# Graph attention on one core: more buffers for the terms of q, loads and one-hots moved, and last units begun in idle buffers

## The chip, the core and the metric

The kernel runs on one NeuronCore of a Trainium2 chip. The core has five engines, each with its own instruction stream: TensorE (PE, matrix products), VectorE (DVE, elementwise work and reductions), ScalarE (ACT, elementwise work), GpSimd (POOL) and SyncE (SP, which here only issues transfers). Work on different engines meets through semaphores; each stream is worked off in order. Times are microseconds (us) on the device. A time given for a kernel is the median of several runs; the profile is one further execution.

## The reference, cut to what matters

There are N = 12,500 nodes with 128 features and E = 212,500 edges, sorted by destination. Eight heads have 16 features each.

```
h   = relu(layernorm(x))
q,v = h Wq' + bq,  h Wv' + bv          per node
k   = edge_attr Wk' + bk               per edge
three logits per edge and head:  q[src].k,  q[dst].k,  q[src].q[dst]   (each times 1/4)
score = sum of their three softmaxes over the edges of a destination, times edge_weight**lam
out = x + leaky_relu( (sum over a node's edges of score * v[dst]) Wo' + bo, 0.1 )
```

Since v is taken at the destination, it is constant within a node's sum: a node needs only the sums of weighted and of plain exponentials for its 24 logits (three kinds of eight heads), and its own v.

## The kernel before

Edges are cut into 416 blocks of 512. The blocks form five streams (S = 5) of neighbouring edges; a step t takes one block of each stream, so there are T = 84 steps and 420 block slots, numbered g = 5 t + s. On each engine the order of work is the order in which the program writes it: `pin` ties each instruction to the one before it on its engine.

**First stage (from the start to about 88 us).** The nodes' rows are loaded, normalized, turned and multiplied by Wq (`statistics`, `scale`, `rectify`, `turn_h`, `nodes_q`), and q is stored to `q_table` in DRAM. Between these groups of four node tiles stand pieces of edge work (`edges_1` to `edges_4`): source indices are turned, and the destination's place within a block (`rel_d`) and flags and weights (`fa_d`) are stored to DRAM. Afterwards the program starts the gathers of the first nine blocks (`gather`, line 625: four indirect transfers of 128 rows of q a block, issued by POOL) and the loads of edge features of the first six blocks (`fetch_edges`).

**Terms of q (about 85 to 155).** `terms_q` writes each value of q as a sum of three bf16 terms: ACT casts (line 845), DVE subtracts (846), ACT casts the rest (851), DVE subtracts (852), and SP stores the group's 384 KB to `q3_table` (854). This is done for 25 groups of four tiles in tiles `q3` with three buffers. In the middle (g = 12) `edges_5` stands in one piece: a reduction (756), a product (758) and four turns of 104 columns into `ends`.

**Main loop.** For a block, PE turns the edge features (`turn`, 1068) and multiplies them by Wk (`project`, 1076 and 1078). The destination's q needs no gather: destinations are sorted, so a window of 42 nodes from `q3_table` (`win`) is spread over the block's edges by a product with one-hots (`spread_q`, 1087), which ACT makes from `relb` (`one_hots`, 1062 and 1063). ACT copies the spread rows to the gathered tile `qq` (1089). DVE forms the three products and their sums over 16 features (`logits`, 1097, 1098, 1100). Once per step, for all five blocks together: the logits are turned (`turn_logits`), a running maximum is taken (`scan_max`: 1130, 1133), ACT takes exponentials (`powers`, 1141 to 1146; PE spreads the weights, `att_ps`, 1148), DVE runs two sums (`scan_sums`: 1154, 1158), marks the last edge of each node (`select`, 1167), and PE and ACT turn the sums back (`turn_sums`) and pick the nodes' rows (`to_rows`, 1191 and 1196), which SP stores to `sums` in DRAM (`put_rows`).

POOL's gathers run LOOK = 9 blocks ahead, in QQ = 11 buffers of `qq`. Gather g waits for products of block g - 9, which keeps it close behind them:

```
if (g - LOOK, j) in behind:
    tc.add_manual_dep(rows.ins, behind[g - LOOK, j], ...)
```

SP's queue holds, in the program's order, the edge loads six blocks ahead, the loads of a step two steps ahead (`fetch`: relb, five fa, register loads, five win), the row stores and the nodes' loads and stores. PSUM tiles of the small parts share three buffers (`small`).

**Nodes.** A unit is 256 nodes; an object `Nodes` holds two. Twenty pairs are finished inside the loop, from step 18 on (`nodes_between`): load sums and x, normalize (970), scores (976 to 981), turn (985, 987), product with Wv, weigh (997), turn, product with Wo, then slope and addition: ACT copies (1007), DVE takes max(0.1 o, o) (1008) and adds x (1009). The nine units left (18, 9, 10, 19, 28, 29, 38, 39, 48; five `Nodes`) are done after the loop, in PSUM tiles of their own (h_ps, v_ps, u_ps, o_ps); six of these nine have sums from two streams, the second loaded into `more` and added (963). Their x is loaded during the last five block slots of the loop.

Of the kernel before, what the change touches and what calls it, by code (L numbers as in the profile page):

```python
# [20 lines left out]
SLOPE = 0.1  # L21
# [451 lines left out]
def ordered_path(ctx: ExitStack, tc: tile.TileContext, flag, x, src, dst, edge_attr, edge_weight,  # L473
# [134 lines left out]
    qqs, st, eas, behind = {}, {}, {}, {}  # L608
# [40 lines left out]
    with tc.tile_pool(name="prep", bufs=1) as prep, \  # L649
# [52 lines left out]
        def turn_edges(of, to):  # L702
            cols = of.rearrange("r (a p j) -> r a j p", a=RB, j=JN)
            for a in range(RB):
                t_ps = prep_ps.tile([P, JN, RW], F32, name="t_ps")
                for j in range(JN):
                    pin(nc.tensor.transpose(t_ps[:, j, :], cols[:, a, j, :], ident[:RW, :RW]))
                pin(nc.vector.tensor_copy(to[:, a:NB:RB, :], t_ps.rearrange("p j r -> p r j")))
# [10 lines left out]
        def of_tile():  # L719
            return prep.tile([RW, RC], BF, name="of", bufs=2)  # L720
# [13 lines left out]
        def edges_3():  # L734
# [6 lines left out]
            rel_b = prep.tile([RW, RB, BE], BF, name="rel_b")  # L741
# [11 lines left out]
        def edges_5():  # L753
            bad = got["bad"] = prep.tile([RW, 1], F32, name="bad")
            step = got["step"]
            pin(nc.vector.tensor_reduce(bad, step[:, :RC], AX.X, ALU.min))
            last = step[:, 1:]
            pin(nc.vector.scalar_tensor_tensor(last, last, 0.0, rel, op0=ALU.is_gt, op1=ALU.mult))
            turn_edges(last, ends)
# [79 lines left out]
        def terms_q(g):  # L839

            if g < GN:
                n = len(tiles_of(g))
                q = xq[:, g * JN:g * JN + n, :]
                q3 = q3s[g] = node.tile([P, JN, 3, F], BF, name="q3", bufs=3)[:, :n]
# [45 lines left out]
        for g in range(AHEAD):  # L890
            fetch_edges(g)
        for g in range(GN + 1):
            terms_q(g)
            if g == GN // 2:
                edges_5()
# [30 lines left out]

    fin = ctx.enter_context(tc.tile_pool(name="fin", bufs=2))
# [11 lines left out]
    class Nodes:  # L939
# [3 lines left out]
        def __init__(self, of):  # L943
            self.of = of
            self.n = 2 * len(of)

        def load_x(self):
            self.x = fin.tile([P, JN, F], F32, name="x_in", bufs=5)
# [3 lines left out]
        def load_sums(self):  # L952
            self.ab = fin.tile([P, JN, 2 * H3], F32, name="ab", bufs=3)
            for i, u in enumerate(self.of):
                for j, t in enumerate(parts_of(u)):
                    to = self.ab
                    if j > 0:
                        to = self.more = fin.tile([P, JN, 2 * H3], F32, name="more", bufs=3)
                    pin(nc.sync.dma_start(to[:, 2 * i:2 * i + 2, :].rearrange("p k c -> p (k c)"),
                                          units(sums[t], u, 1, 2 * H3)[:, 0, :]))  # L960
                    if j > 0:
                        both = self.ab[:, 2 * i:2 * i + 2, :]
                        pin(nc.vector.tensor_add(both, both, to[:, 2 * i:2 * i + 2, :]))

        def normalize(self, lo, hi):
            if lo == 0:
# [6 lines left out]
        def scores(self):  # L973
            n = self.n
            den, num = self.ab[:, :n, 0:H3], self.ab[:, :n, H3:]
# [7 lines left out]
        def turn(self, to):  # L983
            for b in range(self.n):
                pin(nc.tensor.transpose(to[:, b, :], self.h[:, b, :], ident))  # L985
            self.hT = fin.tile([P, JN, P], F32, name="hT")
# [8 lines left out]
        def project_v(self, to):  # L995
            self.product(to, bv3, wv)
            pin(nc.vector.tensor_mul(  # L997
# [5 lines left out]
        def project_o(self, to):  # L1003
# [3 lines left out]
            pin(nc.scalar.copy(o, to[:, :n]))  # L1007
            pin(nc.vector.scalar_tensor_tensor(o, o, SLOPE, o, op0=ALU.mult, op1=ALU.max))  # L1008
# [19 lines left out]
    with tc.tile_pool(name="work", bufs=2) as work, \  # L1028
            tc.tile_pool(name="scan", bufs=2) as scan, \
            tc.tile_pool(name="ps", bufs=1, space=PSUM) as ps:  # L1030
        ks, eTs, qds, lTs, base_v = {}, {}, {}, {}, {}
        end = S * T

        def block_rows(t):
            lo = t if t < G else t - 1
            return lo, slice(0, S * G) if t < G else slice(1, S * G + 1)

        def fetch(t):

            if t >= T:  # L1040
                return
            at, part = block_rows(t)
            relb = load.tile([K3, S, BE], BF, name="relb")
            pin(nc.sync.dma_start(relb, rel_d[part].rearrange("(s b) e -> s b e", b=G)
                                  [None, :, at, :].to_broadcast([K3, S, BE])))
            fa = load.tile([4 * S, BE], BF, name="fa", bufs=4)
            for s in range(S):
                pin(nc.sync.dma_start(fa[4 * s:4 * s + 4], fa_d[s * G + t]))
            _, base_v[t] = nc.values_load_multi_w_load_instructions(
                bases[0:1, t, 0:S], engines=[mybir.EngineType.SP], min_val=0, max_val=N - 1,  # L1050
                skip_runtime_bounds_check_because="the indices of nodes are below N")
            win = load.tile([K3, S, F], BF, name="win")
            for s in range(S):
                pin(nc.sync.dma_start(win[:, s, :], q3_table[bass.ds(base_v[t][s] * 3, K3), :]))
            st[t] = dict(relb=relb, fa=fa, win=win)

        def one_hots(t, s):

            if s == 0:
                st[t]["oh"] = work.tile([K3, S, BE], BF, name="oh")  # L1060
            d = st[t]["relb"][:, s, :]
            pin(nc.scalar.activation(d, d, AF.Abs, bias=before[:K3]))  # L1062
            pin(nc.scalar.activation(st[t]["oh"][:, s, :], d, AF.Relu, bias=1.0, scale=-1.0))  # L1063
# [19 lines left out]
        def spread_q(g):  # L1083
            s, d = g % S, st[g // S]
            qd_ps = ps.tile([P, JN, F], F32, name="qd_ps")
# [264 lines left out]
```

## Time and profile before

| | us |
|---|---|
| median of 3 runs | 2341.86 (2341.75 to 2342.19) |
| the profiled execution's own time | 2333.37 |
| its span, first to last instruction | 2331.5 |

| engine | busy us | share of the span |
|---|---|---|
| DVE | 2150.8 | 92% |
| PE | 1812.6 | 78% |
| POOL | 1658.1 | 71% |
| ACT | 1522.1 | 65% |

A busy share is a mean over stages. In the listings in order of time a line has the start, the duration, the engine, the program's line, the operation, what is written and read, and in brackets how long the engine sat idle before it and what released it. A stretch lists, after its length, the busy time of PE, of weight loads, DVE, ACT and POOL with counts, then PE's granted clock as a share of full, the mean share of the DMA engines, and GB/s. A wait is put down to the releaser that came last; of two merged in one row it may name the wrong one. The issue of a transfer is not counted as busy on SP, but a gather's preparation is on POOL.

### The profile page before, as it was taken

The page shows a single profiled execution, that of the slowest core. Times are in us where ns is not written, and L with a number is a line of the kernel's source. Part 1 is how long each engine was busy: PE and PEld are TensorE (multiplying, and loading weights), DVE is VectorE, ACT ScalarE, POOL GpSimd, SP SyncE. Part 2 cuts the span into 40 slices and gives each one's busy share as a digit, 9 for nine tenths or more (in the row PEclk, how much of TensorE's full clock was granted, in tenths as well). Part 3 has the DMA queues.
Part 4 walks back from the last instruction along what each step waited for, and adds up shares of the span by engine and source line. Part 5 has one row for each costly group of instructions (what it writes and reads, how often), then busy time and mean ns, then how long its engine had stood idle before and what let it go on. Part 6 is the DMA issues. An engine that isn't in the chain of part 4 may idle for free. (4 is left out here: it accounts for less than half of the span.)

```text
span 2331.5 us, 35994 instructions
## 1 busy us (share of the span) xinstructions
PE 1812.6 (78%) x10629; PEld 1415.8 (61%) x10629; DVE 2150.8 (92%) x2263; ACT 1522.1 (65%) x2797; POOL 1658.1 (71%) x1715
## 2 busy tenths in 40 slices
PE   5327888888788888878878778888887777888775
PEld 4315666666666666666666566666666666666654
DVE  7659999999999999999999999999999999999983
ACT  5547676666766676666676676667666667667653
POOL 3547777777777777777777777777777777777740
PEclk9757777777778787787777787778687888688777
DMA  7657545555555555555555655554555554554522
GB/s 201 215 172 197 148 135 148 143 144 149 141 136 159 138 141 163 139 139 154 146 138 139 164 138 140 156 144 137 158 142 140 153 154 135 153 154 134 149 54 60
DMA packets 306681, 341.04 MB, mean 146 GB/s; under 512 B 137667, under 2 KB 225496, under 8 KB 306165
## 3 DMA queue, kind: packets, MB, share of 16 engines
q1 hardware_dynamic: 244906, 222.99, 32.5%
q0 software_dynamic: 54448, 112.96, 19.9%
q10 hardware_dynamic: 7120, 2.70, 0.4%
q8 instruction: 85, 1.39, 0.2%
q14 instruction: 122, 1.00, 0.1%
HBM read 307.79 MB, written 30.64 MB: 145 GB/s over the span
## 5 line engine op out<-in xcount | busy, mean ns | idle before, releaser
L625 POOL DMA_INDIRECT qq<-q_table,src_i x1680 | 1623.4, 966 | 548.6 <-issue 341.4
L1100 DVE TENSOR_REDUCE lT<-prod 128x96 f32<-128x1536 f32 x420 | 736.2, 1753 | 14.4
L1078 PE MATMUL k_ps<-wk,eT 128*128 128x128 f32 x3360 | 613.3, 338 | 103.6 <-ACT eT L1070 95.4
L1078 PEld LDWEIGHTS k_ps<-wk,eT 128*128 128x128 f32 x3360 | 518.9, 236 | 263.7 <-ACT eT L1070 180.9
L1089 ACT COPY qq<-qd_ps 128x512 f32<-128x512 f32 x420 | 245.4, 584 | 548.9 <-PE qd_ps L1087 432.2
L1098 DVE TENSOR_TENSOR prod<-qq,k_ps 128x1024 f32<-128x1024 f32 x420 | 509.8, 1214 | 0.5 <-PE k_ps L1078 0.5
L1087 PE MATMUL qd_ps<-win,oh 126*128 126x128 bf16 x1680 | 203.4, 257 | 213.4 <-DVE prod L1097 173.1
L1068 PE MATMUL eT_ps<-ident,ea 128*128 128x128 f32 x1680 | 342.0, 341 | 2.9 <-DVE found L901 2.9
L1097 DVE TENSOR_TENSOR prod<-qq,qd_ps 128x512 f32<-128x512 f32 x420 | 284.3, 677 | 47.4 <-ACT qq L1089 34.6
L1087 PEld LDWEIGHTS <-oh 126*128 126x128 bf16 x1680 | 159.5, 116 | 257.5 <-issue 208.4
L1062 ACT ACTIVATE relb<-relb,before 126x512 bf16<-126x512 bf16 x420 | 306.3, 729 | 7.4 <-DMA relb<-rel_d 7.4
L1070 ACT COPY eT<-eT_ps 128x512 f32<-128x512 f32 x420 | 246.9, 588 | 50.3 <-PE eT_ps L1068 48.7
L1063 ACT ACTIVATE oh<-relb 126x512 bf16<-126x512 bf16 x420 | 264.6, 630 | 13.4
L1068 PEld LDWEIGHTS eT_ps<-ident,ea 128*128 128x128 f32 x1680 | 243.0, 181 | 3.2 <-DVE found L901 3.2
L1178 PE MATMUL b_ps<-ident,sum 120*128 120x120 f32 x672 | 141.1, 342 | 94.8 <-ACT l L1120 92.3
L1076 PE MATMUL k_ps<-b,ones 3*128 3x512 bf16 x420 | 190.8, 454 | 5.0 <-DVE prod L1098 4.8
L1191 PE MATMUL w_ps<-back,sel 128*126 128x144 f32 x1344 | 186.9, 295 | 0.6 <-ACT back L1179 0.6
L1178 PEld LDWEIGHTS b_ps<-ident,sum 120*128 120x128 f32 x672 | 101.3, 215 | 138.6 <-ACT l L1120 111.4
L1191 PEld LDWEIGHTS w_ps<-back,sel 128*126 128x126 f32 x1344 | 178.4, 197 | 0.8 <-ACT back L1179 0.8
L1179 ACT COPY back<-b_ps 128x480 f32<-128x480 f32 x168 | 97.6, 581 | 47.0 <-PE b_ps L1178 47.0
L1130 DVE TENSOR_TENSOR_SCAN u<-l,u,far_ps 120x512 f32<-120x512 f32 x83 | 105.5, 1271 | 0.8 <-ACT l L1120 0.8
L1158 DVE TENSOR_TENSOR_SCAN sum<-keep,sum,up 120x512 f32<-120x512 f32 x83 | 105.9, 1276 | 0.0
(170 smaller groups left out, 1735.4 us busy)
## 6 DMA issues: line engine op xcount, KB each, us to landing
ea<-in_edge_attr_dram SPq DMA_DIRECT2D x419, 256.0 KB
relb<-rel_d SPq DMA_DIRECT2D x84, 630.0 KB
qq<-q_table,src_i POOLq DMA_INDIRECT x1680
win<-q_table SPq DMA_DIRECT2D x420, 31.5 KB
q_table<-q SPq DMA_DIRECT2D x24, 384.0 KB
fa<-fa_d SPq DMA_DIRECT2D x420, 4.0 KB
sums<-rows SPq DMA_DIRECT2D x416, 7.9 KB
q_table<-xq SPq DMA_DIRECT2D x24, 256.0 KB
```

Source lines behind the costliest of these rows:

```text
L625: rows = pin(nc.gpsimd.indirect_dma_start(out=qq[:, j, 0, :], out_offset=None, in_=q_table, in_offset=bass.IndirectOffsetOnAxis(ap=src_i[: ...
L1062: pin(nc.scalar.activation(d, d, AF.Abs, bias=before[:K3]))
L1063: pin(nc.scalar.activation(st[t]["oh"][:, s, :], d, AF.Relu, bias=1.0, scale=-1.0))
L1068: pin(nc.tensor.transpose(eT_ps[:, j, :], eas[g][:, j * F:(j + 1) * F], ident))
L1070: pin(nc.scalar.copy(eT, eT_ps))
L1078: pin(nc.tensor.matmul(k_ps[:, j, :], eTs[g][:, j, :], wk, start=False, stop=(j == JN - 1)))
L1087: pin(nc.tensor.matmul(qd_ps[:, j, :], d["oh"][:, s, j * P:(j + 1) * P], d["win"][:, s, :], start=(j == 0), stop=(j == JN - 1)))
L1089: pin(nc.scalar.copy(qqs[g][:, :, 1, :], qd_ps))
L1097: pin(nc.vector.tensor_mul(prod[:, :, 2, :], qqs[g][:, :, 0, :], qds[g]))
L1098: pin(nc.vector.tensor_mul(prod[:, :, 0:2, :], qqs[g], ks[g][:, :, None, :].to_broadcast([P, JN, 2, F])))
L1100: pin(nc.vector.tensor_reduce(lTs[t][:, :, s, :], prod.rearrange("p j i (h d) -> p j (i h) d", d=DIM), AX.X, ALU.add))
L1191: pin(nc.tensor.matmul(w_ps[:, i].rearrange("p s c -> p (s c)"), d["sel"][:, j, lo:lo + 3, :].rearrange("p s w -> p (s w)"), d["back"][:, ...
```

## The change

The parts, in order of the program:

- `q3` has four buffers of its own and takes every third group in one of the two buffers of `of` (made 128 partitions tall); `rel_b` uses `of` too, in place of a tile of its own.
- `edges_5` is cut into six pieces, one after every third group of `terms_q`.
- `fetch` is split: relb, fa and the register loads in `fetch`, the win loads in `fetch_rows`. `fetch(0)` stands ahead of `terms_q`.
- At the start of the loop one block's one-hots are made ahead of the first spread, in place of five; `project(0)` and `spread_q(0)` stand ahead of `turn(1)`. In the loop one-hots are made three blocks ahead, in place of five, in five tiles of one block in place of two of five.
- `att_ps` stands first in `powers`, and `powers` ahead of `to_rows`.
- In `project_o` ACT multiplies by the slope while it copies, and DVE takes the maximum against PSUM.
- The nine last units are begun from nine slots before the loop's end (`begin_rest`): their x, h, hT and later their sums lie in buffers of `qq` that no gather uses any more; their products with Wv are kept in PSUM tiles of the loop (`held`), one per slot from the first slot after the last block. After the loop only sums, scores, weighing, the turn, the product with Wo and the store are left; the second sums are loaded on ACT's queue.

```diff
+    def fetch(t):
+        if t >= T:
+            return
+        at, part = block_rows(t)
+        relb = load.tile([K3, S, BE], BF, name="relb")
+        pin(nc.sync.dma_start(relb, ...))
+        fa = load.tile([4 * S, BE], BF, name="fa", bufs=4)
+        for s in range(S):
+            pin(nc.sync.dma_start(fa[4 * s:4 * s + 4], fa_d[s * G + t]))
+        _, base_v[t] = nc.values_load_multi_w_load_instructions(
...
+        st[t] = dict(relb=relb, fa=fa)
+
+    def fetch_rows(t):
+        if t >= T:
+            return
+        win = st[t]["win"] = load.tile([K3, S, F], BF, name="win")
+        for s in range(S):
+            pin(nc.sync.dma_start(win[:, s, :], q3_table[bass.ds(base_v[t][s] * 3, K3), :]))
...
-            rel_b = prep.tile([RW, RB, BE], BF, name="rel_b")
+            rel_b = of_tile().rearrange("r (a e) -> r a e", a=RB)
...
+        def edges_5(i):
             step = got["step"]
             last = step[:, 1:]
+            if i == 0:
+                bad = got["bad"] = prep.tile([RW, 1], F32, name="bad")
+                pin(nc.vector.tensor_reduce(bad, step[:, :RC], AX.X, ALU.min))
+            elif i == 1:
+                pin(nc.vector.scalar_tensor_tensor(last, last, 0.0, rel, op0=ALU.is_gt,
+                                                   op1=ALU.mult))
+            elif i < 2 + RB:
+                turn_edges(last, ends, [i - 2])
...
-                q3 = q3s[g] = node.tile([P, JN, 3, F], BF, name="q3", bufs=3)[:, :n]
+                if g % 3 == 2:
+                    q3 = prep.tile([P, JN, 3, F], BF, name="q3", tag="of", bufs=2)
+                else:
+                    q3 = node.tile([P, JN, 3, F], BF, name="q3", bufs=4)
+                q3 = q3s[g] = q3[:, :n]
...
+        fetch(0)
         for g in range(GN + 1):
             terms_q(g)
-            if g == GN // 2:
-                edges_5()
+            if g % 3 == 2:
+                edges_5(g // 3)
...
-            pin(nc.scalar.copy(o, to[:, :n]))
-            pin(nc.vector.scalar_tensor_tensor(o, o, SLOPE, o, op0=ALU.mult, op1=ALU.max))
+            pin(nc.scalar.activation(o, to[:, :n], AF.Copy, scale=SLOPE))
+            pin(nc.vector.tensor_max(o, o, to[:, :n]))
             pin(nc.vector.tensor_add(y, o, y))
...
+        def one_hots(g):
+            if g < end:
+                oh = ohs[g] = work.tile([K3, BE], BF, name="oh", bufs=5)
+                d = st[g // S]["relb"][:, g % S, :]
+                pin(nc.scalar.activation(d, d, AF.Abs, bias=before[:K3]))
+                pin(nc.scalar.activation(oh, d, AF.Relu, bias=1.0, scale=-1.0))
...
+        starts, holds = (0, 1, 3, 4, 6), ("eT_ps", "eT_ps", "k_ps", "k_ps", "qd_ps")
+        late, turned = {}, {2: (0, 1), 5: (2, 3), 7: (4,)}
+        def spare():
+            return gath.tile([P, JN, 2, F], F32, name="qq").rearrange("p j i f -> p (j i f)")
+        def halves():
+            return spare().rearrange("p (i j f) -> i p j f", i=2, j=JN)
+        def begin_rest(at):
+            if at in turned:
+                late.update(zip(turned[at], halves()))
+            if at in (LOOK - 1, LOOK):
+                late[at - LOOK] = spare()
+            for r, (of, begin) in enumerate(zip(rest, starts)):
+                if at == begin:
+                    to, of.h = halves()
+                    of.load_x(to)
+                if at == begin + 2:
+                    of.normalize(0, 4)
+                if at == begin + 3:
+                    of.hT = late[r]
+                    of.turn(small([P, JN, P], "node_ps"))
+                if at == LOOK + r:
+                    of.held = ps.tile([P, JN, F], F32, name=holds[r], bufs=2 if r < 4 else 1)
+                    of.product(of.held, bv3, wv)
...
-        fetch(0)
+        fetch_rows(0)
         fetch(1)
-        for s in range(S):
-            one_hots(0, s)
+        fetch_rows(1)
+        one_hots(0)
         turn(0)
+        project(0)
+        spread_q(0)
         turn(1)
-        spread_q(0)
-        project(0)
+        one_hots(1)
+        one_hots(2)
         for g in range(end + 2 * S):
...
-            if t + 1 < T:
-                one_hots(t + 1, s)
+            one_hots(g + 3)
...
             elif s == 2:
+                later(powers, t - 1)
                 later(to_rows, t - 2)
-                later(powers, t - 1)
             elif s == 3:
                 later(scan_sums, t - 1)
-                if t + 2 < T:
-                    fetch(t + 2)
+                fetch(t + 2)
+                fetch_rows(t + 2)
...
             nodes_between(t, s)
+            begin_rest(g - (end - LOOK))
...
+        for r, of in enumerate(rest):
+            of.load_sums(*[late[k][:, r * JN * 2 * H3:(r + 1) * JN * 2 * H3].rearrange(
+                "p (j c) -> p j c", j=JN) for k in (-1, 0)])
+        for r in range(len(rest) + 2):
+            if r < len(rest):
+                rest[r].scores()
+                rest[r].weigh(rest[r].held)
+            if 0 <= r - 1 < len(rest):
+                rest[r - 1].turn(small([P, JN, P], "node_ps"))
+            if 0 <= r - 2:
+                rest[r - 2].project_o(small([P, JN, F], "node_ps"))
+                rest[r - 2].store()
```

## The prediction, made before the changed kernel ran

> **What bounds it.** I read the busy shares by stage first: VectorE (DVE) is busy 96 to 98% in the long middle and 40 to 70% at both ends.
>
> ```profile
> 100.00:120.00 20.00, 0.00 (x0) 0.00 (x0) 11.19 (x19) 9.12 (x17) 15.43 (x16) 0.50 0.68 220
> 140.00:160.00 20.00, 0.00 (x0) 0.00 (x0) 12.53 (x33) 7.06 (x14) 6.01 (x6) 0.50 0.66 210
> 300.00:400.00 100.00, 82.88 (x486) 64.24 (x486) 97.97 (x90) 69.47 (x124) 75.91 (x80) 0.78 0.51 141
> 2280.00:2300.00 20.00, 11.21 (x48) 8.05 (x47) 6.99 (x23) 8.04 (x20) 0.31 (x1) 0.67 0.40 109
> ```
>
> (Columns: stretch, length, busy us of PE, weight loads, DVE, ACT, POOL; clock, DMA share, GB/s.) DVE's 97.97 suggests DVE. POOL's 75.91 misleads: 80 gathers per 100 us are all that fit. In order of time POOL reads:
>
> ```profile
> 91.66 1.08 POOL L625 DMA_INDIRECT qq<-q_table,src_i  x1 [10.94 <-DMA ea<-in_edge_attr_dram]
> 146.59 0.94 POOL L625 DMA_INDIRECT qq<-q_table,src_i  x1 [0.30 <-issue]
> 173.73 0.94 POOL L625 DMA_INDIRECT qq<-q_table,src_i  x1 [26.20 <-PE k_ps L1078]
> 174.98 0.95 POOL L625 DMA_INDIRECT qq<-q_table,src_i  x1 [0.30 <-PE eT_ps L1068]
> 2251.76 0.94 POOL L625 DMA_INDIRECT qq<-q_table,src_i  x1 [0.30 <-issue]
> ```
>
> A gather takes 0.94 and 0.30 follows: 1.25, four to a block, 5.0. From 173.73 to 2252.70 POOL never waits beyond this 0.30: 1640 gathers in 2078.97, 1.268 each. So **gather issue is the bound of the loop**; DVE needs less: by the pitches of its rows 3.5 a block plus 5.8 per five blocks (scans 1.9 and 3.0, sel 0.9), so 4.7, and 5.05 where Nodes add 1.85 per five; it trails the gathers. The only hole is 147.53 to 173.73: gather 41, the first of block 10, waits for the products of block 1 (look-ahead of 9).
>
> Next the waits of the stage ahead: 33.8 us of ACT's waits there are for q3_table stores, three q3 buffers.
>
> ```profile
> ACT q L845 <- DMA q_table<-q: 33.8, 21, 8.4
> ```
>
> Then the end, on DVE:
>
> ```profile
> 2262.06 1.75 DVE L1100 TENSOR_REDUCE lT<-prod 128x96 f32<-128x1536 f32 x1
> 2274.03 0.69 DVE L1154 TENSOR_TENSOR ew<-up,att_ps 120x512 f32<-120x512 f32 x1 [5.89 <-ACT up L1145]
> 2292.50 0.26 DVE L963 TENSOR_TENSOR ab<-ab,more 128x96 f32<-128x96 f32 x1 [13.15 <-DMA more<-sums]
> 2323.92 0.42 DVE L1009 TENSOR_TENSOR x_in<-h,x_in 128x256 f32<-128x256 f32 x1 [0.46 <-DVE h L1008]
> ```
>
> The last block's reduce ends near R = 2263.7; the tail from R to 2331.5 is 67.8.
>
> **Start, part by part.** Six q3 buffers for three. Stores now pace 2.28 each (two per 4.56, the casts at 102.06 and 106.90 among others), with or without gathers beside them, so latency sets it. Doubled, latency allows 1.14; DVE needs 1.20 (two subtractions at 0.60 pitch); DMA: stores took 167 GB/s at about 0.48 share (0.68 less 0.20, the gathers' queue's 19.9% in the queue table), so 0.8 share gives 280 GB/s, 1.40 for 384 KB. I take 1.5, DMA-bound; ends 1.4 and 2.28. Splitting the step on ends removes its cluster (119.97 to 128.50, a gap in the stores); its 7 us of DVE fit in the slack, 24.5 x 1.2 + 7 = 36.5 against 24.5 x 1.5 = 36.8.
>
> The first loads (relb, five fa, register loads) go ahead of the stores on SP: 0.54 + 1.93 + 1.3 = 3.8 of issue, 630 KB of transfer, so the first store leaves at 95.5 for 91.5. Last store issued 95.5 + 36.8 = 132.3, landed 135 (2.8 each now). Then only five win loads precede: landing 3.8 after issue at most (159.46 to 163.22), 139. In place of 7.4 of waiting for relb and ten one-hot instructions (161.8 to 168.2), PE does one spread (0.6), a turn (1.06), copies and project(1) (2.7): products of block 1 at **144** for 173.4; DVE starts at 140 for 169.8.
>
> POOL is then not ready: 40 gathers take until 147.5. Here a rule speaks against the change: the Trainium skill, GPSIMD Engine Reference, Specifications, says that POOL shares its SBUF interfaces with DVE and contends with DVE instructions that have two SBUF inputs. The trace agrees, instruction by instruction:
>
> ```profile
> 122.42 2.98 POOL L625 DMA_INDIRECT qq<-q_table,src_i  x1 [0.30 <-issue]
> 122.28 2.29 DVE L758 SCALAR_TENSOR_TENSOR step<-step,dst_r 104x2048 f32<-104x2048 f32 x1
> ```
>
> Over all 1680 gathers, those that begin inside such an instruction are longer than 0.94 by 40 us together (sel 20.9, gap 7.5, terms' subtractions 4.1, L1008 2.3, L758 2.0); those inside one with a PSUM input by nothing. Packed subtractions: 49 x 0.6 / 1.25 = 24 gathers hit, at 0.24 (17 hit now cost 4.1), 5.8 for 4.1: gather 41 at **149**. By the row alone (contention as now) 147.5; I take 149. The start gives POOL 173.7 - 149 = **24.7**. Five us of cover remain; the stall returns once stores exceed 1.7.
>
> **Loop.** The new slope step: ACT scales in its copy (0.58 as before), DVE takes the maximum against PSUM (0.68, as L1097, for 0.68). Its only worth is the 2.3 of gather time that L1008 cost. The rest costs nothing while gathers bound:
> One-hots, same two instructions (1.36), three blocks ahead for five: ACT is 69% busy; without that cover, 1.36 a block. Relb's buffer is now released at a block's second step, just before SP asks for it; SP then sits 9.3 per five blocks (728.3 over 78 waits) at win anyway. Powers (2.1 of ACT) ahead of rows: rows are late by 2.1, the rows' stores on SP come two blocks later; behind them wait edge loads six blocks ahead. In early staging rel_b shares the `of` buffers; POOL's casts may slip 2, ahead of a 10.94 wait.
>
> In the last nine blocks SP waits for an idle qq buffer before loading x (edge loads behind it have four blocks' room); the memset of unit 48 stands behind the last gather on POOL, and its x load, with row stores nobody awaits behind it, lands about 3 later, ahead of its normalization. Five x 0.4 x 4 of ACT and 18 transposes (some 4.5 of PE) enter nine blocks of 5: I charge 1. Loop end: 24.7 + 2.3 - 1 = **26** earlier.
>
> **Tail.** Powers ahead of rows would let ew start at about R + 7 for R + 10.3. But PE is given five products before that chain's end, two ahead of att_ps. From the trace:
>
> ```profile
> 2263.87 1.11 PE L1113 MATMUL l_ps<-ident,lT 128*120 128x128 f32 x4 [6.82 <-DVE lT L1100]
> 2268.38 3.62 PE L1191 MATMUL w_ps<-back,sel 128*126 128x144 f32 x16
> 2272.79 1.16 PE L992 MATMUL node_ps<-wo,hT 128*128 128x128 f32 x8
> 2278.60 3.71 PE L1191 MATMUL w_ps<-back,sel 128*126 128x144 f32 x16 [0.65 <-ACT back L1179]
> ```
>
> A product costs 1.5 at full clock (with its bias), 2.6 at half. The Trainium skill, TensorE: Matmul & The Clock Gate, Part 1, says some 3.4 us of sustained work restore full clock; here PE restarts at 2263.87 and the granted clock stays 0.50 to 2270, 0.64 over 2270:2272, so 7.4. By the page the first product is warm and everything after 3.5 earlier; I take the row: cold to R + 7.5. PE then: l, far, b to R + 3.7; last unit's turn 4.2; product 6.8; turn 7.8; product 9.4; att 9.8 (ew at R + 10.2, gain nothing); w_ps 2.1 warm, 11.9; three products (1.5, 1.5, 0.9) and the old pair's (1.5), 17.3; b_ps 18.8; copy 19.4; w_ps 21.5; rows R + 22 for R + 20.7.
>
> From rows to the first score it is 8.1 now (2284.44 to 2292.50: SP's issue of five row stores, one x load, two ab and one more, then 3.6 to land). The x load (0.25) goes, and the second sums (0.42) to ACT's queue: 7.4, R + 29.4 for 28.8. Then DVE alone: per Nodes scores 2.0 (2292.50 to 2294.5), weigh 0.6, max and add 1.3, 18 for four and a half; the v products and turns that it waited among are gone. I add 1.8 where the first output product (turn 1.06, copy 0.58, cold 2.7, ACT 0.58) is late, and 2.5 of drain at the end: R + 51.7 for R + 60.6; the 7.2 from there to the span's end stay. Tail **8.9** shorter, between 0 (PE cold throughout: 9 more) and 13.
>
> **Sum:** 26 + 8.9 = 34.9 of the profiled 2333.37 (span 2331.5): 2298.5. The runs' median is 8.5 above that execution, so I subtract from the median: 2341.86 - 34.9 = **2307**.
>
> **Rivals.**
> (1) The buffers don't help: stores keep 2.28 (the DMA queues, not latency). Last store 95.5 + 55.9 = 151.4, products of block 1 at 163, the start gives 10.7 for 24.7: 2321. For: 384 KB are large; against: share 0.68, and 306 GB/s at 90:95.
> (2) The early products only move: PE stays cold through the tail, rows at R + 31, the tail gives nothing: 2316. For: the clock was 0.5 to 0.77 in most of 2262:2300; against: PE would have no gap.
> (3) Slower: PE becomes the loop's bound. It is busy 82.9 of 100 at clock 0.78; after the reordering a lower clock would have it pass the gathers' 5.07 a block: it takes the 34.9 back (1.7% of the loop's 2075) where the mean clock falls to 0.636 (0.78 x 0.829 / 1.017), and at 0.63 (2.6%, 55 us) it ends at 2362. Against: PE's order changes little, and fuller PE ran warmer.
>
> **Chances.** Likeliest case 0.63, 2307 (its own 2299 to 2313); (1) 0.13; (2) 0.17; (3) 0.04; 0.03 for still faster (2294). To hold 0.8 the range needs the first, most of (2), some of (1): 2297 to 2320. A measurement tells about 0.2%, 4.7 us: faster 0.94, same 0.02, slower 0.04.
>
> **What would show it.** Gather 41 near 149 with no wait above 0.3 (right) or a wait for k_ps (stores too slow); stores about 1.5 apart; first L1097 near 140; last gather near 2226; no gather longer than 0.94 inside the maximum; ew still some 10 after the last reduce, and w_ps near 2.1; last add about 52 after it. The prediction is wrong if gathers wait in mid-loop, or if DVE's lag behind the last gather (11 to R) grows.

## The result and the profile after

The changed kernel takes **2306.3 us** (median; 2304.05 to 2308.75) where the kernel before, measured beside it, takes 2342.03: a ratio of 0.9844, 95% interval 0.983 to 0.9859, 35.7 us. The forecast was 2307.0. The profiled execution of the changed kernel took 2308.75 (span 2307.0), 2.4 above its median, while that of before lay 8.7 below its own (2342.03); so the two traces show only 24.6 of the 35.7, and a total is compared below by medians, a stage by traces. In the runs e1 to e8 below each engine paused for some 1 to 5 us about every 12 us of the loop, for every kernel (before: 2915 to 2933), so that of them only the stages outside the loop and ratios on the same chip are read.

Three of the stretches shown for before, with the same columns (stretch, length, busy us of PE, weight loads, DVE, ACT, POOL; granted clock, DMA share, GB/s):

```profile
100.00:120.00 20.00, 3.93 (x17) 2.72 (x17) 16.52 (x29) 14.71 (x27) 15.73 (x15) 0.50 0.96 337
300.00:400.00 100.00, 83.57 (x481) 64.13 (x481) 97.76 (x89) 67.51 (x121) 76.29 (x78) 0.77 0.51 148
2280.00:2300.00 20.00, 14.01 (x55) 10.08 (x55) 14.26 (x36) 5.49 (x10) 0.00 (x0) 0.59 0.14 46
```

While the terms of q are stored, all transfers together now move 337 GB/s at a share of 0.96 where they moved 220 at 0.68, and DVE is busy 16.52 of 20 us where it was 11.19. The middle is as it was; the gain lies at the two ends. ACT's 33.8 us of waits for q3 stores have shrunk to this row of the waits:

```profile
ACT q L880 <- DMA q_table<-q: 6.5, 2, 5.8
```

POOL in order of time, with the first gather, the second, gather 41 (153.24: the first that has to wait for products, here those of block 1) and the last:

```profile
93.87 7.29 POOL L652 DMA_INDIRECT qq<-q_table,src_i  x1 [10.71 <-DMA ea<-in_edge_attr_dram]
101.47 0.97 POOL L652 DMA_INDIRECT qq<-q_table,src_i  x1 [0.30 <-issue]
...
153.24 0.94 POOL L652 DMA_INDIRECT qq<-q_table,src_i  x1 [0.30 <-DVE prod L1119]
...
2236.62 0.95 POOL L652 DMA_INDIRECT qq<-q_table,src_i  x1 [0.30 <-issue]
```

The hole of 26 us is gone: gather 41 follows its forerunner by the usual 0.30 and starts 20.5 earlier than before (173.73). It could be 6 us earlier still, for the first gather took 7.29 where it took 1.08 before. The loop's 1640 gathers then take 1.271 each (before 1.268), none waiting beyond 0.32.

The end, on DVE: the last block's last sum ("last reduce"), the product `ew` of exponentials and weights, the first step of the last units' scores ("first score"), and the last addition:

```profile
2247.22 1.75 DVE L1122 TENSOR_REDUCE lT<-prod 128x96 f32<-128x1536 f32 x1
...
2259.27 0.69 DVE L1176 TENSOR_TENSOR ew<-up,att_ps 120x512 f32<-120x512 f32 x1 [5.99 <-ACT up L1169]
...
2276.01 0.26 DVE L1014 TENSOR_TENSOR qq<-qq 128x96 f32<-128x96 f32 x1 [8.40 <-DMA qq<-sums]
...
2299.17 0.43 DVE L1053 TENSOR_TENSOR qq<-qq 128x256 f32<-128x256 f32 x1
```

With R = 2248.9 (the reduce's end, 2247.22 plus a pitch of 1.67): ew at R + 10.4, first score at R + 27.1, last add ending at R + 50.7, the span's end at R + 58.1, for 67.8 before. The tail is 9.7 shorter. In the traces the start gives 20.5 and the tail 9.7, and the loop between takes 5.4 back.

### The profile page after: what moved, and what is told of

Read it like the earlier page. It is cut to its first block, busy times and chain, and to the rows that moved or that the text cites. A ratio compares the mean times of both kernels' runs of the same rounds, so it can differ in the third digit from the quotient of the medians.

```text
span 2307.0 us, 36031 instructions
## 1 busy us (share of the span) xinstructions
PE 1816.2 (79%) x10629; PEld 1395.9 (61%) x10629; DVE 2148.9 (93%) x2263; ACT 1515.6 (66%) x2797; POOL 1666.3 (72%) x1715
## 4 chain that ended last, share of the span: by engine, by line
DVE 26%; PE 24%; ACT 16%; issue 16%; DMA 13%; POOL 4%; SPq 1%; DVEq 0%; ACTq 0%; POOLq 0%
DMA qq<-q_table,src_i 10%; PE k_ps L1099 8%; DVE prod L1120 6%; DVE prod L1119 6%; POOL qq L652 4%; PE eT_ps L1089 4%; DVE sum L1180 4%; PE qd_ps L1108 4%; ACT eT L1091 3%; ACT l L1142 3%; ACT relb L1083 3%; PE b_ps L1200 3%; ACT oh L1084 3%; DVE sel L1189 2%; ACT qq L1110 2%
## 5 line engine op out<-in xcount | busy, mean ns | idle before, releaser
L1099 PE MATMUL k_ps<-wk,eT 128*128 128x128 f32 x3360 | 603.7, 334 | 66.2 <-ACT eT L1091 58.6
L1099 PEld LDWEIGHTS k_ps<-wk,eT 128*128 128x128 f32 x3360 | 510.3, 232 | 217.0 <-ACT eT L1091 146.1
L1089 PE MATMUL eT_ps<-ident,ea 128*128 128x128 f32 x1680 | 332.3, 334 | 12.7 <-DVE found L937 12.7
L1089 PEld LDWEIGHTS eT_ps<-ident,ea 128*128 128x128 f32 x1680 | 234.8, 176 | 13.0 <-DVE found L937 13.0
L1200 PE MATMUL b_ps<-ident,sum 120*128 120x120 f32 x672 | 147.7, 356 | 91.6 <-ACT l L1142 91.6
L1213 PEld LDWEIGHTS w_ps<-back,sel 128*126 128x126 f32 x1344 | 171.9, 191 | 22.3 <-issue 14.2
```

The costliest lines, as they stand in the source:

```text
L1089: pin(nc.tensor.transpose(eT_ps[:, j, :], eas[g][:, j * F:(j + 1) * F], ident))
L1099: pin(nc.tensor.matmul(k_ps[:, j, :], eTs[g][:, j, :], wk, start=False, stop=(j == JN - 1)))
L1200: pin(nc.tensor.transpose(b_ps[:, j, :], d["nd"][i][:, j:BE:JN], ident[:R, :R]))
L1213: pin(nc.tensor.matmul(w_ps[:, i].rearrange("p s c -> p (s c)"), d["sel"][:, j, lo:lo + 3, :].rearrange("p s w -> p (s w)"), d["back"][:, ...
```

## Experiments

**The kernel before, once more (e1).** No edit.

> The kernel before, profiled once more, because its first profile (2333.37 us) lay 8.5 below its median of 2342 and because its gathers were 0.94 us where those of the changed kernel were 0.95. Theory A (the gather's own duration differs a little between executions or chips, and 1680 of them carry it to the end, since gather issue is the bound): either gathers of 0.95 and a span near 2340, or 0.94 and near 2331; duration of a gather and span go together, about 8 us of span for 0.005 us. Theory B (the change itself slows the gathers): again 0.94 and the stages of the first profile.

2924.43. Most gathers took 0.944 as in the first profile, at a pitch of 1.60, so this run decides between the theories not at all: the pauses drown a hundredth of a microsecond. Against the second theory speaks e5 below, the changed kernel again, where the commonest length is 0.944 too (0.947 in its first profile): the change doesn't lengthen the gathers. Why the profile of before lies 8.7 under its median stays open.

**One half at a time (e2, e3).** e2 is the kernel before with the start's edits; e3 the kernel before with the last units begun early, powers and slope as they were.

```diff
 e2, against the changed kernel (parts taken back):
...
-            pin(nc.scalar.activation(o, to[:, :n], AF.Copy, scale=SLOPE))
-            pin(nc.vector.tensor_max(o, o, to[:, :n]))
+            pin(nc.scalar.copy(o, to[:, :n]))
+            pin(nc.vector.scalar_tensor_tensor(o, o, SLOPE, o, op0=ALU.mult, op1=ALU.max))
...
+                later(to_rows, t - 2)
                 later(powers, t - 1)
-                later(to_rows, t - 2)
...
-            begin_rest(g - (end - LOOK))
...
 e3, against the kernel before:
...
             nodes_between(t, s)
+            begin_rest(g - (end - LOOK))
...
```

> Only the start of the change: six q3 buffers, first loads ahead of the terms, edges_5 in pieces, the new order at the head of the loop, one-hots three blocks ahead. Last units, powers and slope as before. Theory A (gather issue bounds the loop, the hole of 26 us in the gathers goes): 18 to 25 us faster than before, no gather waiting over 0.3 us, the tail after the last reduce 68 us as before. Rival (VectorE bounds the loop): VectorE begins its first product 30 us earlier, so 30 us faster.

> Only the last units begun early, in idle buffers, with their sums on two queues; start, powers and slope as before. Theory A: the tail after the last reduce falls from 68 to about 58 us, 9 to 10 us faster; the sum of this run and of the start alone is the whole change. Rival (the early products only move): 0 to 2 us faster.

e2: ratio 0.996 (0.9947 to 0.9973), some 11 us, gather 41 at 159.09 after a wait of 7.81 where none over 0.3 was expected: the windows' loads were issued only from 146.18 on, and five of them took 10.27 for 2.50 in the changed kernel. Its 25 stores took 34.99 from the first issue to the end of the last, those of e1 65.39; tail 65.7 (e1: 65.4). e3: 0.9984 (0.9973 to 0.9995), some 5 us for the 9 to 10 expected, gather 41 at 175.99, tail 58.2 after the last reduce. So the shorter tail belongs to the units begun early: 58.2 with the old order of powers, 58.1 with the new. With the old order ew came at R + 13.4 for R + 10.4, yet the first score at R + 26.4 for 27.1: 3 us of ew bought nothing. The loop's gain can't be judged here.

**Three buffers (e4).** All other edits kept.

```diff
-                if g % 3 == 2:
-                    q3 = prep.tile([P, JN, 3, F], BF, name="q3", tag="of", bufs=2)
-                else:
-                    q3 = node.tile([P, JN, 3, F], BF, name="q3", bufs=4)
+                q3 = node.tile([P, JN, 3, F], BF, name="q3", bufs=3)
```

> The changed kernel with three q3 buffers of its own again and none of the others; all else as changed. Theory A (the latency of three stores set the pace of the terms): stores 2.3 us apart again, the terms end some 20 us later, gather 41 waits about 10 to 14 us for products, and the kernel loses 9 to 14 of the 36 us. Rival (moving the first loads ahead and cutting edges_5 gave the gain): it loses under 4 us.

The 25 stores take 58.71 us from the first issue to the last's end, 32.09 in the changed kernel, and gather 41 waits again:

```profile
163.54 0.94 POOL L652 DMA_INDIRECT qq<-q_table,src_i  x1 [16.05 <-PE k_ps L1096]
```

The buffers make the pace of the stores: 58.71 with three and 34.99 with six (e2), on the same chip and with the same start otherwise. The other edits of the start have their share: gather 41 comes at 163.5 for the 175.3 of e1, beside a first gather that took 1.08.

**Once more, and the start alone (e5, e6).** e5 has no edit, e6 is e2's kernel.

> The changed kernel as it is, beside the kernels below. Theory A (the start frees the gathers some 20 us earlier, the tail is some 9 to 10 us shorter): the same ratio as before, 0.984, some 36 us. In the profile gather 41 near 153 without a wait, the loop's gathers at 1.26 to 1.27 us each, the last add 51 us after the last reduce. Theory B (part of the 36 us is a matter of one execution or one chip): a ratio outside 0.981 to 0.987.

> The kernel before with the changes of the start alone (six buffers of q3, the first loads ahead, the step on ends in pieces, one-hots three blocks ahead); the last nine units, the powers and the slope step stay as before. Theory A (gather issue bounds the loop, so that what gather 41 gains is kept to the end): gather 41 at 153 without a wait for 173.7, 20 us faster than before, and the old tail, 67.8 after the last reduce. Theory B (something later in the loop takes part of it back): less than 15 us, with a wait of POOL in the loop or a longer lag from the last gather to the last reduce. Theory C (the tail gives nothing by itself, all comes from here): 30 us or more.

e5 0.9958 (0.9934 to 0.9982), e6 0.9993 (0.9983 to 1.0004): with the pauses the start's gain dissolves in the loop (the last reduce of e6 lies 1.3 ahead of e5's, while e6 has the tail of before). Three of e5's stages agree with the changed kernel's: first gather 7.70, ew at R + 9.9, the span's end at R + 58.0. Gather 41 does not: it came at 159.16 after a wait of 7.37 (e6: 158.31, 7.34), where one near 153 without a wait was expected, since the first five window loads took 12.28 to issue (e6: 16.11), as in e2. The same kernel's first profile has no such wait; e11 repeats e6.

**The pieces of `edges_5` six groups later (e7).**

```diff
-            if g % 3 == 2:
-                edges_5(g // 3)
+            if g % 3 == 2 and g >= 8:
+                edges_5(g // 3 - 2)
```

> The changed kernel with the pieces of the step on ends begun six groups later, when the first gathers are under way. Theory A (the first gather took 7.3 us for 1.1 because the first two pieces, with two inputs in SBUF, and the packed subtractions followed each other on VectorE while it started): the first gather back to 1 to 3 us, gather 41 at 148 to 150 without a wait, 4 to 6 us faster than the changed kernel. Theory B (the back-to-back subtractions alone held it, or the collision only moves to later gathers): the first gather still above 5 us, or other gathers longer by as much; within 2 us of the changed kernel.

Ratio 0.9955 (0.9933 to 0.9976) beside e5's 0.9958. Theory B: the first gather is free, and the collision moves and grows. POOL:

```profile
93.31 1.08 POOL L652 DMA_INDIRECT qq<-q_table,src_i  x1 [11.16 <-DMA ea<-in_edge_attr_dram]
...
108.09 11.30 POOL L652 DMA_INDIRECT qq<-q_table,src_i  x1 [0.30 <-issue]
119.70 3.81 POOL L652 DMA_INDIRECT qq<-q_table,src_i  x1 [0.31 <-issue]
```

And DVE over the same time: the piece in which that gather starts, then packed subtractions and L787, and the first instructions that read PSUM:

```profile
106.87 2.28 DVE L785 TENSOR_REDUCE bad<-step 104x1 f32<-104x2048 f32 x1
109.07 0.68 DVE L881 TENSOR_TENSOR xq<-xq,q 128x512 f32<-128x512 f32 x1
...
117.89 0.68 DVE L887 TENSOR_TENSOR q<-xq,q 128x512 bf16<-128x512 f32 x1
118.49 0.58 DVE L735 COPY ends<-t_ps 128x416 f32<-128x416 f32 x1
...
122.60 0.58 DVE L735 COPY ends<-t_ps 128x416 f32<-128x416 f32 x1
```

The gather of 108.09 ends at 119.39, 0.8 after the last subtraction's end (118.57); the next at 123.51, 0.8 after the next L735 has relieved the subtractions. From 109.07 to 118.57 DVE ran instructions with two SBUF inputs without a pause, and this gather did not end before them; two more after 119.70 took 3.80. But such a run does not hold every gather, as e12 shows below. Gather 41 came at 166.08.

**A quarter of the gathers taken out (e8, e10).**

```diff
-            for j in range(JN):
+            pin(nc.sync.dma_start(qq[:, JN - 1, 0, :], q_table[(g % 90) * P:(g % 90 + 1) * P, :]))
+            for j in range(JN - 1):
```

> The changed kernel with the fourth gather of every block replaced by one plain load of 128 fixed rows of q on SP's queue, of the same size: a quarter of the gathered q is of other nodes; all other work is as in the changed kernel. Theory A (the issue of gathers is the loop's bound, 5.08 us a block): POOL would need 3.8 a block, and VectorE, idle 4% of the loop (65 us of the 1600 from 400 to 2000), or TensorE takes over: the loop at 4.88 to 5.0 a block, 30 to 80 us faster than the changed kernel, and VectorE's waits for the gathered rows gone. Theory B (VectorE is the bound, as its 96% suggest, and the gathers only keep pace): within 10 us of the changed kernel, with POOL waiting in the loop.

> Once more the changed kernel with the fourth gather of every block replaced by a plain load of 128 fixed rows of q on SP's queue (a quarter of the gathered q is of other nodes), since the chip of the first time stopped all engines again and again. Theory A (the issue of gathers bounds the loop, 5.08 us a block): on an undisturbed chip POOL needs 3.8 a block and waits, VectorE's 65 us of waits over 400 to 2000 shrink, the loop goes to 4.85 to 5.0 a block: 30 to 80 us faster than the changed kernel, 2230 to 2275. Theory B (VectorE is the bound at 96% and the gathers keep pace with it): within 10 us of the changed kernel, 2297 to 2317. Theory C (the transfer of the rows, not their issue, is the bound, as the loads carry the same bytes): also within 10 us, with VectorE waiting for the loaded rows.

e8: ratio 0.8475 (0.8449 to 0.8501), far beyond either theory. Why a quarter of the gathers is worth that much beside the pauses stays open, and it doesn't tell what bounds the loop without them. e10, the same edit without pauses: 2285.25 (its trace 2294.15), ratio 0.9752 (0.9728 to 0.9777), 21 us below the changed kernel. In the waits of e10 from 400 to 2000 (what waited for what: us in total, times, longest) POOL has room, and DVE hardly waits for rows:

```profile
POOL qq L653 <- issue: 348.7, 581, 4.6
...
DVE prod L1120 <- ACT qq L1111: 25.8, 40, 1.7
...
DVE prod L1120 <- DMA qq<-q_table,src_i: 2.6, 3, 0.9
```

In the changed kernel the last of these was 21.9 (18 times, longest 3.1). So B (within 10) falls, and so does C, since the loads carried the same bytes. A holds in kind, not in size: 21 for 30 to 80. The blocks of 121 to 420 follow each other, by the reduces, at 5.04 in e10's trace and 5.10 in the changed kernel's (5.05 before, where DVE's lag from the end of a block's last gather to the end of its reduce still shrank from 15.3 to 11.1 on the way): freed from the gathers, the loop is at once held by something else at 5.04. DVE is busy over 96% of that time, and its lag behind the gathers, 42 to 53, neither grows nor shrinks for long, so it is DVE that holds it, as far as a trace can tell.

**The step on ends (`edges_5`) behind the terms (e12), and the held products behind the last block's rows as well (e9).**

```diff
 e9 and e12:
             terms_q(g)
-            if g % 3 == 2:
-                edges_5(g // 3)
+        edges_5(0)
...
         pin(nc.vector.tensor_copy(top_f, tops))
+        for i in range(1, 2 + RB):
+            edges_5(i)
 e9 alone:
-                if at == LOOK + r:
+                if at == LOOK + S + 2:
```

> The changed kernel with two edits that lie at its two ends, so that stage times tell them apart: the whole step on ends stands behind the terms of q, in VectorE's pause before the first products (its first piece right behind the terms, the others behind the casts of the bounds check), and the five held products come after the last block's rows have been put together. Start, theory A (a gather that begins among back-to-back VectorE instructions with two inputs in SBUF is held to the first pause, plus its own 0.95; in the run with the pieces six groups later the gather at 108.09 ended 0.95 after such a pause): without pieces among the terms VectorE's run is broken earlier, the first gather takes 1 to 3.5 us for 7.3 and gather 41 comes at 148 to 151 where nothing else stops. Theory B (a gather beside the terms of q is held whatever stands among them): 6 us or more. Tail, theory C (TensorE's queue sets it: the products ahead of the last block's chain delay ew and rows): ew at R + 7 to 8 for R + 10, rows by R + 18 to 19 for R + 22, the first score 3 to 4 us earlier and the span's end at R + 54 to 55 for R + 58. Theory D (a cold TensorE or ACT's order sets it, the products only fill a gap): ew and first score within 1 us, or the held products late for the scores; the end at R + 57 or later. Time: 4 to 8 us faster than the changed kernel by A and C, 2 us at most by B and D.

> The changed kernel with only the first of the two edits of the run with the ends last: the step on ends behind the terms of q; the held products stay where the change put them. That run was 13.6 us faster than the changed kernel, and by its stage times 9 of them came from gather 41 and 5 from the tail. Theory A (the stage times add up): first gather under 3.5 us, gather 41 at 144 to 150, the tail of the changed kernel (58 after the last reduce), 5 to 10 us faster than the changed kernel, 2296 to 2301. Theory B (the earlier gathers only lengthen VectorE's lag, and the products' place brought nearly all): within 4 us of the changed kernel, 2302 to 2310.

e12 takes 2297.92 (0.981; 0.9785 to 0.9835), e9 **2292.66** (0.9798; 0.9775 to 0.9822): 8.4 and 13.6 below the changed kernel (their runs, 2293.7 to 2301.12 and 2290.33 to 2297.33, lie wholly below its 2304.05 to 2308.75). In e12 the first gather takes 1.17; its POOL and, later, its DVE:

```profile
144.73 0.94 POOL L652 DMA_INDIRECT qq<-q_table,src_i  x1 [0.30 <-PE k_ps L1100]
```

```profile
141.47 0.69 DVE L1120 TENSOR_TENSOR prod<-qq,qd_ps 128x512 f32<-128x512 f32 x1 [3.84 <-ACT qq L1111]
```

Gather 41 is 8.5 earlier than in the changed kernel, while DVE's first product is 3.6 *later* (137.85 there), since the step on ends now fills DVE's pause. And the kernel is 8.4 faster. That is the plainest evidence for what bounds the loop: what counted was when the gathers ran, not when DVE began.

e12 also shows a long run of DVE that holds almost nothing. From 102.18 to 125.97 DVE worked off 39 subtractions without a pause, all with two SBUF inputs; 19 gathers began in that time, and 18 of them took 0.94 to 0.96 (one 1.33). One of them, and the subtraction that began with it:

```profile
108.35 0.94 POOL L652 DMA_INDIRECT qq<-q_table,src_i  x1 [0.30 <-issue]
```

```profile
108.35 0.72 DVE L881 TENSOR_TENSOR xq<-xq,q 128x512 f32<-128x512 f32 x1
```

The tail of e9 by DVE, and by PE:

```profile
2234.38 1.75 DVE L1123 TENSOR_REDUCE lT<-prod 128x96 f32<-128x1536 f32 x1
...
2243.48 0.69 DVE L1177 TENSOR_TENSOR ew<-up,att_ps 120x512 f32<-120x512 f32 x1 [3.50 <-ACT up L1170]
...
2258.30 0.26 DVE L1015 TENSOR_TENSOR qq<-qq 128x96 f32<-128x96 f32 x1 [7.96 <-DMA qq<-sums]
```

```profile
2241.19 0.68 PE L1165 MATMUL att_ps<-fa,spread 20*120 20x512 bf16 x1
2241.94 4.21 PE L1214 MATMUL w_ps<-back,sel 128*126 128x144 f32 x16
...
2252.33 1.16 PE L1034 MATMUL eT_ps<-wv,qq 128*128 128x128 f32 x8
```

R is 2236.05: ew at R + 7.4, first score at R + 22.2 (27.1), the span's end at R + 53.0, for 57.8 in e12. Theory C: the products' place cost 5. The medians of e12 and e9, 5.3 apart, point the same way, though the intervals of the two ratios overlap. Without the products PE is at half clock at w_ps (4.21 for 2.23), and it is still the better order.

**The start alone, without pauses (e11).** e2's kernel.

> Once more the kernel before with the changes of the start alone (six buffers of q3, the first loads ahead, the step on ends in pieces, one-hots three blocks ahead), since the chip of the first time stopped all engines again and again; units, powers and slope step as before. Theory A (what gather 41 gains is kept through the loop, since VectorE, which needs 5.04 a block by the run with three gathers, starts earlier too): gather 41 at 150 to 154 for 173.7, 20 to 27 us faster than before, 2313 to 2320, with the old tail of 66 to 68 after the last reduce. Theory B (VectorE, 0.03 a block from being the bound, keeps part of it): 10 to 17 us, with VectorE's lag behind the last gather grown over 11. Theory C (the last units early give nothing, all comes from the start): 33 us or more.

2318.8, ratio 0.9898 (0.9865 to 0.9932): 22 us faster than before (16 to 32 by the interval): theory A by the median, while the interval still reaches into B. Gather 41:

```profile
152.03 0.94 POOL L652 DMA_INDIRECT qq<-q_table,src_i  x1 [0.30 <-DMA qq<-q_table,src_i]
```

The gather is 21.7 earlier, the tail 66.8. DVE's lag from the last gather's end to the last reduce's grew to 15 (11 before), which in this trace is 4 of theory B. The first gather took 7.49 here too.

## Why the prediction was right, and where its terms were off

**The bound.** "Gather issue is the bound of the loop" held: POOL never waits in the loop of the changed kernel, e12 gains with its gathers though DVE begins later, e10 gains by having fewer. What the text passed over lightly is its own second figure, 5.05 a block for DVE where Nodes are worked. It was right (5.04 in e10), and it means that the bound's margin is about 1%: with a quarter of the gathers gone, and POOL waiting, the win was 21 us. DVE's lag from the last gather's end to R is 11.3 in the changed kernel (11.0 before), so it did not grow.

**Stores: 1.5 taken, 1.3 measured** (32.09 for 25). The figure lies below even the lower end of the estimate, 1.4, and the step that failed is the bound, "DMA-bound". The stores alone moved some 300 GB/s (an estimate: 24.5 groups of 393 kB in 32.09 us), more than the 280 that the text allowed, and it was DVE that set their pace: from 107.90 to the end of the terms at 129.16 it runs without a pause, three groups in 4.15 (three pairs of subtractions at some 1.20 and one L735 at 0.50, by their distances), and all of ACT's waits for stores lie ahead of it. So the step on ends found no slack to fit in: in e12, without its pieces among the terms, the stores take 30.40. The first product came at 137.85 for 140 predicted. It costs nothing either way: POOL was the later one, and the products of block 1 (ending at 139.89) were some 13 us ahead of gather 41, in place of 5. Rival (1) falls with it, and e4 shows its case, three buffers.

**Gather 41: 149 predicted, 153.24 measured.** This is the term of the sum that was mis-sized. Of the 4.2, 2.2 is a first stage that ended later (first gather at 93.87 for 91.66). Most of the rest is contention. I priced it at 0.24 for each gather that hits a subtraction, 5.8 over the stage, beside the 2.0 that the product `step` (L758 before, L787 now) cost already: 7.8. The excess over 0.94 or 0.95 was 9.3 over the first 40 gathers, 6.3 of it in one gather and 3.0 in the other 39. So the mean was too dear for most and blind to the one. Here is what it stood behind:

```profile
92.12 2.28 DVE L785 TENSOR_REDUCE bad<-step 104x1 f32<-104x2048 f32 x1
94.32 0.68 DVE L881 TENSOR_TENSOR xq<-xq,q 128x512 f32<-128x512 f32 x1
...
97.33 0.68 DVE L887 TENSOR_TENSOR q<-xq,q 128x512 bf16<-128x512 f32 x1
97.93 2.28 DVE L787 SCALAR_TENSOR_TENSOR step<-step,dst_r 104x2048 f32<-104x2048 f32 x1
103.34 0.69 DVE L881 TENSOR_TENSOR xq<-xq,q 128x512 f32<-128x512 f32 x1 [3.13 <-ACT q L880]
```

Six subtractions and L787 without a pause; DVE stops at 100.21, the gather ends at 101.16. I had put two of the pieces exactly there. The page I cited for it says that the two engines contend; another page of the Trainium skill, SBUF — State Buffer, section "SBUF: two separate sides", says more: the pair of ports is an exclusive lock for a whole instruction, and the other engine fully blocks (for a DVE instruction with two SBUF inputs, where the GpSimd operation reads SBUF). By the sum's rate the e7 gather would have taken 1.2, by a lock for one instruction at most 2.3 more than 0.94; the trace shows 11.30, as if the lock passed from instruction to instruction. And in e12 18 of 19 gathers took their usual time beside such instructions, where a lock on whole instructions would have made one of the two wait. The measurements decide: neither the rate nor the rule forecasts which gather is held. With the pieces away (e12) the start gave 29 us in the trace, more than the 24.7 forecast, so the pieces' place among the terms is part of what held the first gather: with six buffers and the pieces there it took 7.13 to 7.88 in all seven traces, without them (e9, e12) or with them later (e7) under 1.2. Both L785 and a run behind it seem to be needed: in e4 too the first gather began in L785, but DVE paused behind it, and it took 1.08. Why is not shown.

**Loop: 26 predicted for its end, 15.1 in the traces** (last gather's end 2237.57 for 2252.70; near 2226 by the text). Of the missing 11, 4 are gather 41's. The rest is the pitch, 1.271 in this execution for the 1.267 that the sum implied; e12 had 1.267 and e11 1.270. The commonest length of a gather was 0.947 here and 0.944 in before, e11, e12 and e5, the last being the same kernel: 0.003 over 1640 gathers are 5 us, and they lie between executions. e11's 1.270 at 0.944 shows a few thousandths more that the lengths don't explain; no cause in the change is shown. The slope step did what was said: gathers begun inside L1008 were longer by 2.3 us in all before, those begun inside the maximum (L1052) by nothing; its 2 us were not run alone.

**Tail: 8.9 predicted, 9.7 measured.** Term by term, with the measured value in brackets: ew at R + 10.2 (10.4), w_ps 2.1 (2.23), rows at R + 22 (21.8), first score R + 29.4 (27.1), last add R + 51.7 (50.7). PE's order was as written:

```profile
2253.63 2.08 PE L1033 MATMUL eT_ps<-wv,qq 128*128 128x128 f32 x8
...
2257.45 1.35 PE L1033 MATMUL eT_ps<-wv,qq 128*128 128x128 f32 x8
2258.74 0.42 PE L1164 MATMUL att_ps<-fa,spread 20*120 20x512 bf16 x1
2259.09 2.23 PE L1213 MATMUL w_ps<-back,sel 128*126 128x144 f32 x16
```

The product at 2253.63 ran at half clock, and during the next the granted clock rose to full (at 2257.89), some 9 us after PE restarted at 2249.03: the row of before (7.4) was the nearer guide than the 3.4 of the cited page on the clock gate. "Gain nothing" for ew was right and for the stated reason: e9 takes the two products away from in front of att_ps and ew comes at R + 7.4, the "about R + 7" of the text. Rival (2) falls as a whole (w_ps ran at full clock, the tail gave 9.7), but e9 shows a share of it: the products held up the last block's chain by 5.

**The sum.** Start 4 short (20.5 for 24.7), tail 0.8 over, loop's pitch within the spread of executions. The traces give 24.6 of the 34.9, the medians 35.7, and the median came within 0.7 of 2307.0. So close a hit is luck: by the traces the sum is 10 off, and before's execution was 8.7 under its median while this one was 2.4 above. Rival (3) falls: granted clock 0.79, PE 83.57 of 100 in the same stretch.

## What to carry to other kernels

When one engine's issue bounds a loop, move forward what lets that engine run, and put other engines' work where it can't hold it up: here a DVE step of 7 us cost 8 when it stood among the terms of q and nothing when it filled DVE's pause. Don't price contention by a mean per collision alone: here 39 gathers lost 3.0 us together and one lost 6.3, at the head of the chain that bounds the loop. And before paying for a tighter bound, see what the next one needs (5.04 for 5.08 a block here); in a tail, ask which product is needed last and put it last, even if TensorE's clock is lower for it.

## What the runs showed of the hardware that I had not expected

- A gather can be held to the end of a run of DVE instructions with two SBUF inputs, however long: 7.29, 7.70 and 7.49 us in the changed kernel, its repeat and e11, 11.30 in e7, each ending 0.8 to 0.95 after the run. All four, and those of the other traces over 7 us, began in the last part of L785, a reduction with one SBUF input, with such a run behind it. L785 held up nothing by itself: in e9 it ran from 125.47 to 127.74 and the gathers begun at 125.40 and 126.67 took 0.96 and 0.94. It is not the only way: the three of 3.80 and 3.81 in e7 began in a subtraction.
- A long run by itself doesn't hold gathers either: in e12, 18 of the 19 that began amid 39 packed subtractions took 0.94 to 0.96, and the first gathers of e9 and e12 took 1.19 and 1.17 amid a packed run. What decides is open.
- With six buffers the stores moved some 300 GB/s (estimated above) and all transfers together 337, at a DMA share of 0.96, where I had set the limit for the stores at 280.
